# A transformer block with cross-attention on one Trainium2 core: two output tiles moved ahead of the gated layer, and a norm's steps put into every second half unit

## The chip, the cores and the metric

The kernel runs on one core of a Trainium2 chip. The metric is the time of one execution in device microseconds (us). A core has five engines that each work through their own instructions in order: TensorE (PE; its weight loads are PEld), VectorE (DVE), ScalarE (ACT), GpSimd (POOL) and SyncE (SP, which here only starts transfers). They wait for each other by semaphores.

## The reference

The input x has 2 batches of 1024 tokens with 256 features, the context has 2 batches of 154 tokens with 192 features, and all numbers are float32. The block is self-attention, cross-attention and a gated feed-forward layer, each behind a layer norm and each added back to x:

```python
h = _layernorm(x, ln1_g, ln1_b)
x = _attention(h, h, sa_wq, sa_wk, sa_wv, sa_wo, sa_bo) + x
h = _layernorm(x, ln2_g, ln2_b)
x = _attention(h, cond_emb, ca_wq, ca_wk, ca_wv, ca_wo, ca_bo) + x
h = _layernorm(x, ln3_g, ln3_b)
p = h @ ff_w1 + ff_b1
a, gate = (p[..., :D_FF], p[..., D_FF:])
h = a * jax.nn.gelu(gate, approximate=False) @ ff_w2 + ff_b2
return h + x
```

Attention has 16 heads of 64, and D_FF is 1024.

## The kernel before, in words

The order of every instruction is written out by hand: Python closures issue the work, and a few lists hold pieces that are waiting for a place. `tc.manual_schedule()` keeps that order on each engine.

The work has three stages. Self-attention runs in 16 units (2 batches by 8 pairs of heads). Cross-attention follows as 48 steps c, three to a unit. The gated layer follows as 64 half units k (line 1274), with c = 48 + k. The names that matter:

- **The gated layer.** Its tokens are worked in 4 pairs of 256-token blocks, and each pair in 8 units of 128 hidden features; a unit is two half units. The products of a unit are arranged so that seven matrix products of 256 columns serve both token blocks, at the price of sums made ahead: `weight_sums` (L956) and, once for each pair, `token_sums` (L976, four POOL additions L982 to L985). `gate_first` (L1003) issues product 1 into the bank `pa`, then `gate_last` of the unit before (L1045: its last product, into its `pb`), then products 6 and 5 into new `pb` and `pc`. `gate_second` (L1030) adds products 2, 7 and 3 to `pa`, `pb` and `pc`. Beside them stand, for each unit, three ACT instructions (L1018, L1036, L1042), five on DVE (L1022, L1024, L1038, L1041, L1050) and two POOL multiplications (L1043, L1052). They work in a tile `own`, taken from the pool `pp_`, which has 6 buffers and also holds attention weights `p`, the token sums `hs` and the normalised rows `xn`.
- **Results of the gated layer.** From unit 8 on, two product steps `sum_slot` (L1058, output `pf`) are issued in each half unit.
- **What is left of cross-attention.** The weighted values of the last two units of cross-attention (`cross_values`, L861, output `poc`, units 14 and 15) fall into half units k = 1 and k = 5. Their DVE copies go into `o_ca` (L890).
- **Output tiles of cross-attention.** `out_piece` (L457) issues four matmuls of 256 columns into a bank `py_ca`, for two token tiles, and leaves a DVE addition to x (L470) in the list `adds`. Four such pieces make up one quarter (`half`) of the heads for a batch. `out_pieces` puts them in the list `outs`. Quarter 2 of batch 1 needs `o_ca` up to unit 13, quarter 3 up to unit 15.
- **The last norm.** `norm_beside("ff", 1)` (L322), called at k = 7, puts seven steps in the list `side`. A step does, for different pairs of token tiles, the transposition `turn` (four PE transpositions L276 into a bank `ph`, then two ACT instructions L291), `stats` (DVE, L236 and L237, twice), `deviation` (POOL, L242 and L246) and `normalize` (DVE L252, then two POOL instructions L263 that write `xn`). The transposition of a pair comes one step after its `normalize`. An eighth item, `add_biases`, puts eight POOL additions of a bias (L316) in the list `later`. One item is popped from `later` per half unit. The last transposition of batch 0's norm is still in `side` when the gated layer begins.
- **Filling.** At the end of each half unit `run_work(n, n_side, bank, n_sum)` (L559) takes up to `n_side` items from `side`, and up to `n` output tiles from `outs` into banks of the pool `ps_m` (`mm_tile`), with `n_sum` more into banks of the pool `ps_o` (`sum_tile`). A step with transpositions needs a bank: it takes one of the `n`, or `bank` when that is given.
- **The seam.** Before the gated layer the score banks' pool `ps_s` is closed and a pool `ps_f` of four banks opened in its place (L1271 to L1273); `pb` and `pc` come from it. They so follow the last exponentials (ACT, L814) that read the scores of step 47.

The lines that the change touches, before:

```python
if k == 0:
    out_pieces("ca", B - 1, NQ - 2, out_order("ca"))
...
run_work(0 if k == 1 else 1 + k % 2, 1, sum_tile if len(CG) + 2 < k < 2 * NF else None)
```

Of the kernel before, what the change touches and what calls it, by code (L numbers as in the profile page):

```python
# [18 lines left out]
def tile_transformer_block(ctx: ExitStack, tc: tile.TileContext, a: dict, out: bass.AP):  # L19
# [4 lines left out]
    B, S, D = x.shape  # L24
# [5 lines left out]
    NQ = 4  # L30
# [21 lines left out]
    NF = DF // P  # L52
# [45 lines left out]
    for n in names:  # L98
        k = n_of[n]
# [200 lines left out]
    def tile_order(kind):  # L300

        if kind == "ff":
            return list(range(NT))
        return [t for i in range(NT // 2) for t in (i, NT // 2 + i)]
# [17 lines left out]
    def norm_beside(kind, b):  # L322

        after = {"sa": None, "ca": "sa", "ff": "ca"}[kind]
        stats, deviation, normalize, turn = norm_pieces(kind, b)
        n = 1 if narrow(kind, b) else 2
        lag = {}  # L330
        for fns, first in ((turn, 3), (stats, 0), (deviation, 1), (normalize, 2)):
            for i, fn in enumerate(fns):
                t = i if fns is stats else 2 * i + 1
                lag.setdefault(first + t // n, []).append((fn, fns is turn))
        for k in range(NT // n + 3):
            tiles = tile_order(kind)[k * n:(k + 1) * n]
            needs = [(after, b, half, t) for half in range(NQ) for t in tiles if after]

            def step(fns=lag[k]):
                done = [fn() for fn, _ in fns]  # L340
                return next((fn for fn in done if fn), None)

            side.append((any(turns for _, turns in lag[k]), needs, step))
        if not narrow(kind, b):
            side.append((False, (), lambda: add_biases(kind, b)))
# [111 lines left out]
    def out_piece(kind, b, g, t):  # L457

        o = oT[kind, b, g]
        py = spare["out"](f"py_{kind}{b}_{g}_{t}")  # L460
        for e in range(2):
            for i in range(HP):
                nc.tensor.matmul(  # L463
                    py[:, e * D:(e + 1) * D], lhsT=o[:, i, (t + e) * P:(t + e + 1) * P],
                    rhs=wo[kind][:, g * HP + i, :], start=(i == 0), stop=(i == HP - 1),
                )
        xs = xt[b, t // GT][:, t % GT:t % GT + 2, :].rearrange("p t d -> p (t d)")

        def add():
            nc.vector.tensor_tensor(xs, py, xs, ALU.add)  # L470
            added.update((kind, b, g, t + e) for e in range(2))

        add.adds = True
        return add

    def out_order(kind):

        return [t for t in tile_order("ff" if kind == "ca" else "ca") if t % 2 == 0]
# [67 lines left out]
    stores, adds = [], []  # L546
    later = []

    def run(piece):
        done = piece()  # L550
        if done is not None:
            (adds if getattr(done, "adds", False) else stores).append(done)

    def flush(queue):
        for fn in queue:
            fn()
        queue.clear()

    def run_work(n, n_side, bank=None, n_sum=0):  # L559

        while n > 0 and work:
            n -= work[0].banks
            run(work.pop(0))
        for _ in range(min(n_side, len(side))):
            needs_bank, needs, fn = side[0]
            if needs_bank and not bank and n <= 0 or not added.issuperset(needs):
                break  # L570
            if needs_bank and not bank:
                n -= 1
            spare["bank"] = bank or mm_tile
            run(fn)
            side.pop(0)
        for i in range(min(max(n, 0) + n_sum, len(outs))):
            spare["out"] = mm_tile if i < n else sum_tile
            run(outs.pop(0))

    def out_pieces(kind, b, half, tiles):  # L580
        outs.extend(lambda t=t: out_piece(kind, b, half, t) for t in tiles)
# [120 lines left out]
    CG = [(t, min(TG, NT - t)) for t in range(0, NT, TG)]  # L702
# [144 lines left out]
    def cross_regroup(c):  # L847

        ui, n = divmod(c - len(CG) - 2, len(CG))
        if n != 0 or not 0 <= ui < NU:  # L850
            return
        for a2 in range(2):
            for a4 in range(P // KB):
                half, e = divmod(a4, 2)
                own = slice(a4 * KB, (a4 + 1) * KB)
                src = slice((2 * half + a2) * KB, (2 * half + a2 + 1) * KB)
                blocks = pTc["ring"][src, ui % 3, :2 * NM].rearrange("p (m e) j q -> p m e (j q)", e=2)
                nc.sync.dma_start(
                    out=pTc["pairs"][own, a2].rearrange("p m j q -> p m (j q)"), in_=blocks[:, :, e])
# [47 lines left out]
    def cross_drain(c):  # L907

        n = c - 2
        if 0 <= n < CA:  # L910
            cross_turn(n)

    def cross_weigh(c):

        ui, n = divmod(c - 2 * len(CG) - 1, len(CG))
        if n == 0 and 0 <= ui < NU:
            for part in range(2):
                run(lambda: cross_values(ui, part))
            flush(stores)
# [56 lines left out]
    def token_sums(pair):  # L976

        b, t0 = divmod(pair * 2 * BT, S)
        h = hT["ff", b]
        own = [[h[:, c, t0 + j * BT:t0 + (j + 1) * BT] for j in range(2)] for c in range(NC)]  # L980
        t = pp_.tile([P, 3, BT], F32, tag="P", name=f"hs{pair}")
        nc.gpsimd.tensor_tensor(t[:, 0, :], own[0][1], own[0][0], ALU.subtract)  # L982
        nc.gpsimd.tensor_tensor(t[:, 1, :], own[1][1], t[:, 0, :], ALU.subtract)
        nc.gpsimd.tensor_tensor(own[0][1], own[1][1], own[0][1], ALU.subtract)
        nc.gpsimd.tensor_tensor(t[:, 2, :], own[1][0], t[:, 1, :], ALU.subtract)  # L985
        wh[pair] = {
            1: own[0][0], 2: own[1][0], 3: own[1][1], 4: t[:, 2, :],
            5: t[:, 0, :], 6: t[:, 1, :], 7: own[0][1],
        }
# [92 lines left out]
    with tc.manual_schedule():  # L1082
# [98 lines left out]
        for c in range(CA):  # L1181
# [89 lines left out]
        scored.close()  # L1271
        pools["f"] = ctx.enter_context(
            tc.tile_pool(name="ps_f", bufs=4, space=bass.MemoryType.PSUM))  # L1273
        for k in range(2 * FU):
            c = CA + k
            flush(adds)
            (gate_second if k % 2 else gate_first)(k // 2)
            flush(stores)
            flush(lates)
            if k == 2 * len(CG) + 1:  # L1280
                norm_beside("ff", B - 1)
            if k == 0:
                out_pieces("ca", B - 1, NQ - 2, out_order("ca"))
            cross_drain(c)
            if k % 2:
                cross_weigh(c - 1 if k == len(CG) + 2 else c)
            cross_regroup(c)
            if k == len(CG) + 2:
                out_pieces("ca", B - 1, NQ - 1, out_order("ca"))
            if k % (2 * NF) == NF and k < 2 * FU - 2 * NF:  # L1290
                token_sums(k // (2 * NF) + 1)
            for _ in range(min(2, len(sums))):
                run(sum_slot)
            flush(stores)
            run_work(0 if k == 1 else 1 + k % 2, 1, sum_tile if len(CG) + 2 < k < 2 * NF else None)
            if later:
                later.pop(0)()
        gate_last(FU - 1)
# [36 lines left out]
```

## Time and profile before

| what | value |
|---|---|
| median of three runs | 1108.2 us (1106.76 to 1109.0) |
| the profiled execution | 1109.85 us |
| its span, first to last instruction | 1108.1 us |
| mean granted clock of TensorE | 0.995 |
| PE busy in the span | 1081.6 us, 98% |
| POOL busy | 734.0 us, 66% |
| first `pa` of the gated layer | 916.58 us from the span's start |
| first `pf` | 978.25 us |

The gated layer takes the last 191 us of the span. In the views, times are us from the span's start. In the timeline a row is a run of like instructions: start, duration, engine, line, operation, output and inputs, count, and in brackets the idle time of the engine just before it with what seems to have ended it. In the view by windows each engine has its busy time in a stretch, and PEclk is the share of full speed that TensorE's clock was granted in it.

### The profile page before, as it was taken

To read this page: it belongs to the slowest core of one execution; us is meant where nothing else is said; L and a number is where in the kernel's file an instruction comes from. 1 tells how busy PE (TensorE), PEld (TensorE's weight loads), DVE (VectorE), ACT (ScalarE), POOL (GpSimd) and SP (SyncE) were. 2 spreads that over 40 slices of the span, in tenths; PEclk is the share of its full clock that TensorE was granted. 3 is DMA by queue.
4 is the path that set the end of the run, shared out by engine and by line. 5 is a ranking of instruction groups with operands and counts; after the bars stand their busy time and mean duration, and the time that the engine had idled before them with its cause. 6 is when DMAs were issued, how large, how long until landed. Compare 5 with 4: busy or idle time off the path is not lost.

```text
span 1108.1 us, 44904 instructions
## 1 busy us (share of the span) xinstructions
PE 1081.6 (98%) x18388; PEld 718.1 (65%) x18388; DVE 894.2 (81%) x1301; ACT 637.8 (58%) x2057; POOL 734.0 (66%) x1552
## 2 busy tenths in 40 slices
PE   8999999999999999999999999999999999899998
PEld 6555666556756555566565565566766677688887
DVE  5889999898988998999998989878777885544442
ACT  4766666766666666666666766665556553132221
POOL 2767777777778777777777767776656784564331
PEclk9999999999999999999999999999999999999999
DMA  3222212121112021111110111046665543000000
GB/s 82 71 56 56 57 28 52 41 53 42 34 42 49 14 48 37 26 42 33 33 42 23 41 33 27 23 99 162 162 160 138 118 110 77 0 8 12 15 15 29
DMA packets 104094, 60.71 MB, mean 55 GB/s; under 512 B 32330, under 2 KB 94674, under 8 KB 103890
## 3 DMA queue, kind: packets, MB, share of 16 engines
q1 hardware_dynamic: 102514, 57.07, 21.8%
q8 instruction: 145, 2.38, 0.9%
q10 hardware_dynamic: 1376, 0.79, 0.2%
q14 instruction: 59, 0.48, 0.1%
HBM read 27.91 MB, written 2.10 MB: 27 GB/s over the span
## 4 chain that ended last, share of the span: by engine, by line
PE 60%; ACT 10%; DMA 8%; DVE 7%; POOL 6%; SPq 4%; issue 4%; DVEq 0%; POOLq 0%; ACTq 0%
PE s L489 10%; PE po L535 10%; ACT p L500 8%; DMA st<-st 6%; PE pf L1065 5%; DVE st L650 5%; PE py_ca L463 4%; PE pq_ca L358 4%; SPq L510 4%; PE poc L877 4%; PE pb L999 4%; PE py_sa L463 3%; PE sc L798 3%; PE pk_sa L358 3%; PE pa L999 2%
## 5 line engine op out<-in xcount | busy, mean ns | idle before, releaser
L500 ACT ACTIVATE p<-s,st 128x512 f32<-128x512 f32 x512 | 345.4, 687 | 195.6 <-DVE st L650 191.9
L600 POOL TENSOR_SCALAR p<-p,rd,ee 128x512 f32<-128x512 f32 x512 | 387.7, 773 | 47.2 <-DVE rd L596 46.2
L650 DVE TENSOR_REDUCE st<-s 128x2 f32<-128x1024 f32 x256 | 300.8, 1216 | 22.8 <-PE s L489 8.2
L614 DVE STREAM_TRANSPOSE pT<-p 128x1024 f32<-128x1024 f32 x256 | 302.3, 1218 | 0.3 <-POOL p L600 0.3
L489 PE MATMUL s<-k_sa,q_sa 64*32 64x512 f32 x4096 | 261.4, 593 | 7.9 <-ACT p L500 7.0
L535 PE MATMUL po<-pT,v_sa 64*32 64x256 f32 x8192 | 240.6, 376 | 1.9 <-DVE pT L614 1.4
L535 PEld LDWEIGHTS po<-pT,v_sa 64*32 64x32 f32 x8192 | 175.7, 106 | 74.8 <-issue 22.0
L489 PEld LDWEIGHTS s<-k_sa,q_sa 64*32 64x32 f32 x4096 | 82.3, 106 | 111.7 <-ACT p L500 54.6
L814 ACT ACTIVATE p<-sc,neg 128x154 f32<-128x154 f32 x256 | 96.4, 406 | 84.0 <-DVE rden L822 78.9
L825 POOL TENSOR_SCALAR p<-p,rden 128x154 f32<-128x154 f32 x256 | 97.4, 402 | 58.5 <-DVE rden L822 58.2
L500 ACT ACTIVATION_READ_ACCUMULATOR p<-s,st 128x1 f32 x512 | 104.0, 203 | 0.0
L523 POOL TENSOR_TENSOR zz<-ee,st 128x8 f32<-128x8 f32 x128 | 26.0, 203 | 72.0 <-ACT ee L521 72.0
L389 PEld LDWEIGHTS pv_sa<-sa_wv,hT_ln 64*128 64x128 f32 x1024 | 58.8, 188 | 14.6 <-issue 5.9
L389 PE MATMUL pv_sa<-sa_wv,hT_ln 64*128 64x128 f32 x1024 | 62.1, 275 | 0.3 <-ACT v_sa L398 0.3
L518 POOL TENSOR_TENSOR dd<-st 128x8 f32<-128x8 f32 x128 | 25.9, 202 | 53.6 <-DMA st<-st 49.1
L463 PE MATMUL py_ca<-ca_wo,o_ca 128*128 128x256 f32 x256 | 59.9, 382 | 0.5 <-DVE o_ca L890 0.5
L463 PE MATMUL py_sa<-sa_wo,o_sa 128*128 128x256 f32 x256 | 59.7, 385 | 0.0
L463 PEld LDWEIGHTS py_sa<-sa_wo,o_sa 128*128 128x128 f32 x256 | 47.3, 190 | 17.9 <-ACT v_sa L398 6.7
L358 PE MATMUL pq_sa<-hT_ln,sa_wq 64*32 64x512 f32 (+1 forms) x976 | 58.4, 587 | 0.0
L358 PE MATMUL pq_ca<-hT_ln,ca_wq 64*128 64x512 f32 (+1 forms) x304 | 57.9, 590 | 0.0
L358 PE MATMUL pk_sa<-hT_ln,sa_wk 64*32 64x512 f32 x960 | 57.4, 590 | 0.5 <-ACT q_sa L373 0.5
L803 DVE TENSOR_REDUCE neg<-sc 128x6 f32<-128x924 f32 (+1 forms) x48 | 47.9, 999 | 11.8 <-PE sc L798 11.7
(117 smaller groups left out, 1464.3 us busy)
## 6 DMA issues: line engine op xcount, KB each, us to landing
wf<-pT_ca SPq DMA_DIRECT2D x128, 128.0 KB, 2.4
st<-st SPq DMA_DIRECT2D x512, 1.0 KB, 1.8
v_sa<-v_sa SPq DMA_DIRECT2D x32, 256.0 KB, 3.8
sa_wq<-in_L_xattn_sa_wq_dram SPq DMA_DIRECT2D x32, 128.0 KB, 3.4
sa_wk<-in_L_xattn_sa_wk_dram SPq DMA_DIRECT2D x32, 128.0 KB, 2.9
sa_wv<-in_L_xattn_sa_wv_dram SPq DMA_DIRECT2D x32, 128.0 KB, 3.1
ca_wq<-in_L_xattn_ca_wq_dram SPq DMA_DIRECT2D x32, 128.0 KB, 3.7
wf<-in_L_xattn_ff_w_dram SPq DMA_DIRECT2D x12, 256.0 KB
```

The lines of the kernel that those rows point to most:

```text
L358: nc.tensor.matmul(pq[r][f:f + m, at:at + n], lhsT=wt[own, c, f:f + m], rhs=h[own, c, t0:t0 + n], start=(c == 0), stop=(c == NH - 1), tile ...
L389: nc.tensor.matmul(pv[r][:, i * P:(i + 1) * P], lhsT=h[own, c, i * P:(i + 1) * P], rhs=wt[own, c, :], start=(c == 0), stop=(c == NH - 1), ...
L463: nc.tensor.matmul(py[:, e * D:(e + 1) * D], lhsT=o[:, i, (t + e) * P:(t + e + 1) * P], rhs=wo[kind][:, g * HP + i, :], start=(i == 0), st ...
L489: nc.tensor.matmul(sc[a4 * KB:(a4 + 1) * KB, j, :], lhsT=q[r, c:c + KB], rhs=k[r, h * HB:(h + 1) * HB], start=True, stop=True, tile_positi ...
L500: nc.scalar.activation(pr[:, j, :], sc[:, j, :], AF.Exp, bias=st[:, 0, 0, i, j:j + 1], accum_out=st[:, 0, 1, i, j:j + 1],)
L535: nc.tensor.matmul(po[a2][d:d + KB, :QH // 2], lhsT=v[r, t, e, d:d + KB], rhs=pT[r, d // DH * NK + n, :], start=(t == 0 and e == 0), stop= ...
L600: nc.gpsimd.tensor_scalar(pr[:, j, :], pr[:, j, :], rd[:, c:c + 1], ee[:, 0, c:c + 1], op0=ALU.mult, op1=ALU.mult,)
L614: nc.vector.transpose(halves[h][:, :, c:c + KB], groups.pop(0).rearrange("p j (n k) -> p (j n) k", k=KB))
L650: nc.vector.tensor_reduce(st[:, 0, 0, i, :], sc[i], AX.X, ALU.max, negate=True)
L814: nc.scalar.activation(pr_[:, j, i, :T], sc[:, j, i * T:(i + 1) * T], AF.Exp, bias=neg[:, j, i:i + 1], accum_out=den[:, j, i:i + 1],)
L825: nc.gpsimd.tensor_scalar(pr_[:, j, i, :T], pr_[:, j, i, :T], rden[:, j, i:i + 1], 1.0, op0=ALU.mult, op1=ALU.mult,)
L999: nc.tensor.matmul(into[:, :BT], lhsT=lhs, rhs=wh[pair][i], start=first, stop=True, skip_group_check=True)
```

## The change

Two edits, both in the gated layer's loop. The four output pieces of quarter 2 are listed before the loop, and in k = 0 two of them are issued ahead of the first unit, into `sum_tile` banks. `run_work` at the end of a half unit now takes an item of `side` only where k is odd, and never passes a bank, so that a step with transpositions uses one of the `n` banks of `mm_tile`.

```diff
+        out_pieces("ca", B - 1, NQ - 2, out_order("ca"))
+        flush(adds)
         for k in range(2 * FU):
             c = CA + k
+            if k == 0:
+                run_work(0, 0, n_sum=2)
             flush(adds)
             (gate_second if k % 2 else gate_first)(k // 2)
             flush(stores)
             flush(lates)
             if k == 2 * len(CG) + 1:
                 norm_beside("ff", B - 1)
-            if k == 0:
-                out_pieces("ca", B - 1, NQ - 2, out_order("ca"))
             cross_drain(c)
...
-            run_work(0 if k == 1 else 1 + k % 2, 1, sum_tile if len(CG) + 2 < k < 2 * NF else None)
+            run_work(0 if k == 1 else 1 + k % 2, k % 2)
             if later:
                 later.pop(0)()
```

The built order of instructions shows what this moves. No engine gains or loses an instruction, and the order of SP's transfers is the same.

| | before | after |
|---|---|---|
| output tiles of quarter 2 | one in k = 2, two in k = 3, one in k = 4 | two ahead of the first `pa`, one in k = 0, one in k = 2 |
| last transposition of batch 0's norm | k = 0 | k = 3 |
| the eight bias additions for batch 0 | k = 1 to 8 | k = 5 to 12 |
| seven steps of the last norm | k = 7, 8, 9, 10, 11, 12, 13 | k = 7, 9, 11, 13, 15, 17, 19 |
| its four transpositions | after k = 10, 11, 12, 13 | after k = 13, 15, 17, 19 |
| the eight bias additions for batch 1 | from k = 14 | from k = 21 |

## The prediction

> **What bounds the kernel now.** I read the page first, then the view by windows over the gated layer's start, then what TensorE waited for there, then the timeline. The page names the bound:
>
> ```profile
> PE 1081.6 (98%) x18388; PEld 718.1 (65%) x18388; DVE 894.2 (81%) x1301; ACT 637.8 (58%) x2057; POOL 734.0 (66%) x1552
> ```
>
> TensorE is busy for 98% of the span. The change neither adds nor removes an instruction, so it can only win back time that TensorE waits or runs slowly. From 914 to 990 us TensorE's waits are these (waiter, waited for, us in total, times, longest), and after 990 us the same view lists none:
>
> ```profile
> PE ph_ln L276 <- POOL xn_ln L263: 5.6, 4, 3.9
> PE pb L999 <- POOL p L825: 2.0, 1, 2.0
> PE py_ca L463 <- DVE o_ca L890: 0.5, 1, 0.5
> ```
>
> Two places carry nearly all of it, the seam (2.0 us) and the last norm's transpositions (5.6 us). Each has a second price, which the windows show in PEclk:
>
> ```profile
> core 0: us, PE busy (x) PEld busy (x) DVE busy (x) ACT busy (x) POOL busy (x), PEclk, DMA share, GB/s
> 915.60:919.00 3.40, 1.68 (x14) 0.86 (x10) 2.80 (x6) 1.58 (x10) 2.96 (x8) 1.00 0.92 198
> 919.00:922.40 3.40, 3.12 (x9) 2.58 (x10) 1.46 (x5) 1.73 (x4) 2.08 (x6) 0.50 0.49 105
> 960.00:963.40 3.40, 0.27 (x1) 0.14 (x1) 2.89 (x9) 0.00 (x0) 3.24 (x7) 1.00 0.01 2
> 963.40:966.80 3.40, 3.19 (x10) 2.61 (x10) 0.48 (x1) 0.47 (x1) 2.88 (x6) 0.50 0.00 0
> ```
>
> After each stretch in which TensorE was busy for half the time or less, the next 3.4 us ran at half clock. The products there start 0.86 us apart instead of 0.43. Such a stretch costs up to 1.7 us.
>
> The Trainium skill ("TensorE: Matmul & The Clock Gate", section "Why this matters for your kernels") asks for no idle gaps over about 3 us. By that rule the 2.0 us gap at the seam would cost no clock, and the sum below would be 1.6 us smaller; the row at 919.00 speaks against the rule. Its Part 1 calls the window of 3413 ns free-running, so that the same gap need not halve the clock in every run; one trace cannot show that.
>
> **The seam.** The view puts `pb`'s wait down to POOL's L825, which was still running. The program's order says that `pb` needs the bank of step 47's scores, whose last reader on ACT is this:
>
> ```profile
> 918.97 0.21 ACT L814 ACTIVATION_READ_ACCUMULATOR p<-sc,neg 128x1 f32 x1
> 919.28 1.19 PE L999 MATMUL pb<-hs,w1s 128*128 128x256 f32 x2 [2.00 <-POOL p L825]
> ```
>
> It ends at 919.18. Work on TensorE ahead of `pb` hides that wait if it can start early. An output tile takes 1.73 us (start at 929.11, the next product at 930.84), two take 3.46. They need `o_ca` of unit 13, whose last DVE copies L890 (915.59, 0.80 us for two) end at 916.4; the old first `pa` had the same wait, with TensorE's whole queue behind it, and its weight load was held up by 0.16 us. So they start at 916.6, `pa` follows at 920.0 and `pb` at 920.5, 1.3 us after ACT is done. What goes:
>
> - from `pa`'s end at 917.01 (916.58 + 0.43) to 919.28: **2.27 us**;
> - the half clock at 919.0 to 922.4: products 919.28 to 922.62 take 3.34 us. The same `pb`, `pc`, transposition and `pa` take 4 x 0.43 = 1.73 at full clock. **1.6 us**;
> - unit 14's `poc` took from 923.58 to 927.28, 3.70 us; unit 15's, with the wait for `o_ca` behind it, 3.33 (940.43 to 943.76). The excess of **0.4 us** is a weight load that waited for ACT L291, the copy of the transposition in k = 0. That transposition moves to k = 3, and the bank's reader is then a DVE addition that is ready before L1038.
>
> Sum **4.2 us** (2.27 + 1.6 + 0.4, rounded). What the edit adds on other engines is off the path. The two additions L470 (0.69 us each) stand on DVE ahead of L1022, which the first `pb` needs no earlier than 921; the second tile ends near 920.0, so its addition ends near 920.7. At worst the second one delays the first products by its 0.69 us; I take 0. Unit 15's transfers (L858) start when `poc` of unit 14 has read the old data. Their last one starts at 929.6 and takes 2.4 us to land, 4.7 us behind that `poc`'s end at 927.3. The new order has 14 products, one tile and one transposition until unit 15's `poc`, 6.06 + 1.73 + 0.43 = 8.2 us (four tiles and 13.0 us before). So 3.5 us of slack remain; I take 0, and the bound above is the 0.4 us that a wait for such a transfer cost at 914.41.
>
> **The last norm.** Count from unit 3's last product, at 954.23 (the first `pb` after the `pa` at 953.80), to the first `pf` at 978.25: 24.02 us. The work in between is 31 products (3 + 3 of unit 4, 7 each of units 5, 6 and 7, 4 of unit 8) and 4 transpositions at 0.43 each, 15.15 us. So **8.87 us** are lost now, 1.7 of them by the half clock. What the first transposition waits for is GpSimd's queue:
>
> ```profile
> 955.42 0.73 POOL L1052 TENSOR_TENSOR u<-own 128x256 f32<-128x256 f32 x1 [0.70 <-DVE own L1050]
> 956.12 0.73 POOL L982 TENSOR_TENSOR hs<-hT_ln 128x256 f32<-128x256 f32 x1
> ...
> 958.30 0.73 POOL L985 TENSOR_TENSOR hs<-hT_ln,hs 128x256 f32<-128x256 f32 x1
> 959.10 0.19 POOL L242 TENSOR_SCALAR var_ln<-mv_ln 128x2 f32<-128x2 f32 x1
> 959.38 0.71 POOL L246 TENSOR_TENSOR rstd_ln<-var_ln,power 128x2 f32<-128x2 f32 x1
> 960.05 0.72 POOL L316 TENSOR_TENSOR x<-x,ff_b 128x256 f32<-128x256 f32 x1
> 960.74 0.73 POOL L1043 TENSOR_TENSOR kT<-own 128x256 f32<-128x256 f32 x1
> 961.54 0.19 POOL L242 TENSOR_SCALAR var_ln<-mv_ln 128x2 f32<-128x2 f32 x1
> 961.82 0.71 POOL L246 TENSOR_TENSOR rstd_ln<-var_ln,power 128x2 f32<-128x2 f32 x1
> 962.52 1.10 POOL L263 TENSOR_SCALAR xn_ln<-x,rstd_ln,off_ln 128x256 f32<-128x256 f32 x2
> ```
>
> There is no gap in it: from 955.42 to the first transposition at 963.13 are 7.71 us of GpSimd, and 955.42 itself is 1.19 us behind the product at 954.23. Spreading the steps gives TensorE more work ahead of the transposition, but **GpSimd gets more too**. In the new order the queue from unit 3's L1052 to the first `xn` holds all of these and also two more bias additions (batch 0's stand at k = 5 to 12 now), unit 4's L1052 and unit 5's L1043. Each steps 0.69 us (960.05 to 960.74): 4 x 0.69 = 2.76. So the first transposition can start 1.19 + 7.71 + 2.76 = 11.66 us after that product. TensorE has 20 products until then (3 + 3, and 7 each of units 5 and 6), 8.66 us: **3.0 us lost**. Some 0.8 of it shows earlier, as waits of second half units for DVE: a step's `stats` hold DVE for 1.08 us (956.07 to 957.15) and now stand ahead of L1050 and L1022, which had 0.2 us to spare (L1022 ended 955.78, product 7 started 955.96).
>
> From the first transposition to the second's first: GpSimd has the second half of `xn` (0.45), two bias additions, L1052, L1043 (2.76), the step to L242 that is 0.11 longer than 0.69, L242 and L246 (0.28 + 0.70) and half an `xn` (0.61), together 4.91. TensorE has the transposition with its wait for the second half of `xn` (963.13 to 963.67, then 0.32) and 7 products (3.03), 3.89. **1.0 us lost**, and 0.43 (0.54 less the 0.11 that one transposition takes) for the split of each of the two. The third and fourth stand behind `pf` work and without bias additions ahead of them; I take 0 for their waits, the bound above is the 1.3 us of the third one now. Sum lost: 3.0 + 1.0 + 2 x 0.43 = **4.9**.
>
> The new first wait leaves 2.2 + 0.4 us idle close together, about the 2.0 us that halved the clock at the seam, so I give a half-clock stretch 7 in 10. Of its 1.7 us the wait of 1.0 that follows absorbs 1.0, so 0.7 x 0.7 = 0.5. Gain 8.87 - 4.9 - 0.5 = **3.5 us**.
>
> **Sum.** 4.2 + 3.5 = 7.7 us from the profiled execution's 1109.85 gives 1102.2. That execution is 1.65 us above the median of the runs shown, about one half-clock stretch. Taking all 7.7 from 1108.2 gives 1100.5; without the seam's 1.6 it gives 1102.1. I predict **1102 us**.
>
> **Rivals.** Measurement can tell 0.2% (2.2 us) from no change, so faster means below 1106.0 and slower above 1110.4.
>
> - *GpSimd keeps up* (7%): the waits for `xn` vanish and only DVE's 0.8 stays. Gain 4.2 + 8.07 = 12.3, 1097.6. Against it: the queue above has no gap, and its items can be counted.
> - *Only the seam gains* (15%): GpSimd's lag takes back the whole 3.5. 1109.85 - 4.2 = 1105.6. For it: GpSimd has 4.9 us of work in each of units 4 to 6 (two multiplications 1.4, two additions 1.4, a norm step 2.0) against TensorE's 3.03.
> - *The seam's wait only moves* (10%): the tiles start late, or `pb` waits for DVE. 1109.85 - 3.5 = 1106.3. Against it: the same `o_ca` was there for `pa` at 916.58.
> - *Slower* (8%): GpSimd paces TensorE through `own`. Of 6 buffers, two hold `hs` and one `xn`, which now lives two half units. If a new unit's L1018 must wait for a late L1052, TensorE follows the queue to its end: 1.19 us, 10.5 to the first `xn`, 4.9 to the second, 3.6 to the third (L1052 and L1043 1.5, L242 and L246 1.0, `xn` 1.1), then 4.8 for 11 products to `pf`. That is 25.0 against 14.3 of work (31 products, 2 transpositions). Lost 10.7, and with four half-clock stretches, half of them absorbed, 14.1, which is 1.0 more than the 13.1 lost now: 1111. It decides once unit 7's L1018 waits past its product 2. Counted from the first transposition, unit 5's L1052 ends at 0.45 + 0.69 + 0.73 = 1.87 and L1018 0.4 later, 2.3; product 2 is due at 0.54 + 0.32 + 4 x 0.43 = 2.6. Only 0.3 us are to spare.
>
> The forecast has 60%, at 1102 and within about 1099 to 1105. Range **1099 to 1106.5**: it takes in the first case, both one-sided gains, and leaves out about 2 in 10. Faster: 0.60 + 0.07 + 0.11 + 0.03 = 0.81; same 0.11 (rest of the two one-sided cases); slower 0.08.
>
> **What would show it.** Right: no wait of the first `pb`, full clock there; the first transposition after k = 13 waits about 2 us and the second about 1 us for `xn`, with GpSimd busy without a gap from its token sums on; the first `pf` near 970 (954.23 - 4.2 + 14.3 + 4.9 + 0.5). Wrong: a wait of the first output tile; waits of `pa` or of product 2 for L1018; no wait for `xn` at all; any new wait behind the first `pf`.

## The result and the profile after

The changed kernel took **1099.66 us** (median of 4 runs, 1098.1 to 1100.75) against 1107.48 us for the kernel before (4 runs, 1106.61 to 1109.0): ratio 0.9927, 95% interval 0.9908 to 0.9946. The forecast was 1102. Measured again beside later experiments, it took 1100.87 us (6 runs) against 1107.65 (16 runs): 0.9946, interval 0.9929 to 0.9963.

The profiled execution took 1098.87 us, its span 1097.1 us, with a granted clock of 0.998. The page of the changed kernel, its row for the bounding engine:

```profile
PE 1076.0 (98%) x18388; PEld 711.9 (65%) x18388; DVE 893.2 (81%) x1301; ACT 638.1 (58%) x2057; POOL 730.1 (67%) x1552
```

The instructions are as many as before. PE is busy for 5.6 us less (1081.6 before). Of these, 2.9 us lie in the part that the change reorders (185.5 us busy from 904.85 to the end, 188.4 from 907.46 before), 1.6 of them by the half clock at the seam. The other 2.7 lie ahead of it, where the order is the same. What TensorE waits for from 905 to 990 us in the changed kernel (waiter, waited for, us in total, times, longest):

```profile
PE ph_ln L276 <- POOL xn_ln L263: 1.8, 1, 1.8
PE pa L999 <- DVE o_ca L890: 0.5, 1, 0.5
PE py_ca L463 <- DVE o_ca L890: 0.5, 1, 0.5
PE pb L999 <- DVE own L1022: 0.4, 1, 0.4
PE poc L877 <- issue: 0.2, 1, 0.2
```

`pb`'s 2.0 us at the seam is gone, and 5.6 us for `xn` have become 1.8. Behind 990 us the view lists none, as before. The windows of the changed kernel, two at the seam and two at the first transposition:

```profile
core 0: us, PE busy (x) PEld busy (x) DVE busy (x) ACT busy (x) POOL busy (x), PEclk, DMA share, GB/s
913.70:917.10 3.40, 3.40 (x18) 2.97 (x17) 2.61 (x5) 1.59 (x8) 3.16 (x9) 1.00 0.94 202
917.10:920.50 3.40, 3.40 (x17) 3.01 (x16) 2.69 (x6) 1.66 (x2) 1.80 (x6) 1.00 0.29 61
955.00:958.40 3.40, 1.72 (x7) 0.82 (x5) 2.90 (x9) 0.98 (x2) 3.24 (x7) 1.00 0.00 0
958.40:961.80 3.40, 2.86 (x8) 2.23 (x9) 0.39 (x3) 0.54 (x2) 3.40 (x6) 0.53 0.00 0
```

At the seam TensorE is now busy throughout, at full clock. At the transposition it is idle for half of a window, and the next 3.4 us run at half clock. The seam in the timeline of ACT, then of PE:

```profile
916.13 0.21 ACT L814 ACTIVATION_READ_ACCUMULATOR p<-sc,neg 128x1 f32 x1
```

```profile
913.74 3.72 PE L463 MATMUL py_ca<-ca_wo,o_ca 128*128 128x256 f32 x16
917.30 0.59 PE L999 MATMUL pa<-hT_ln,wf 128*128 128x256 f32 x2
917.73 0.59 PE L999 MATMUL pb<-hs,w1s 128*128 128x256 f32 x2
```

The last exponential's sum ends at 916.34, and `pb` needs the bank only at 917.73, 1.4 us later. The two tiles (16 matmuls) fill the time. GpSimd's queue ahead of the first transposition, in its timeline:

```profile
948.45 0.73 POOL L1052 TENSOR_TENSOR u<-own 128x256 f32<-128x256 f32 x1 [0.70 <-DVE own L1050]
949.13 0.73 POOL L982 TENSOR_TENSOR hs<-hT_ln 128x256 f32<-128x256 f32 x1
...
955.80 0.73 POOL L316 TENSOR_TENSOR x<-x,ff_b 128x256 f32<-128x256 f32 x1
956.49 0.72 POOL L1043 TENSOR_TENSOR kT<-own 128x256 f32<-128x256 f32 x1
957.29 0.19 POOL L242 TENSOR_SCALAR var_ln<-mv_ln 128x2 f32<-128x2 f32 x1
957.56 0.70 POOL L246 TENSOR_TENSOR rstd_ln<-var_ln,power 128x2 f32<-128x2 f32 x1
958.27 1.09 POOL L263 TENSOR_SCALAR xn_ln<-x,rstd_ln,off_ln 128x256 f32<-128x256 f32 x2
```

Behind the idle time ahead of 948.45 none is named until `xn`: GpSimd works without a gap. What TensorE does then, in its own timeline:

```profile
958.87 1.44 PE L276 MATMUL ph_ln<-ident,xn_ln 128*128 128x128 f32 x4 [1.78 <-POOL xn_ln L263]
960.11 1.06 PE L999 MATMUL pa<-hT_ln,wf 128*128 128x256 f32 x2
960.96 1.06 PE L999 MATMUL pb<-hs,wf 128*128 128x256 f32 x2
```

The transposition waited 1.78 us for `xn`. Its 1.44 us for four instructions (0.60 for four at full clock), and products 0.85 us apart behind it, are the half clock.

**A yardstick.** Whole times scatter by some us from one execution to the next, much of it ahead of the changed part. So I compare the stretch from the last 16-matmul output product ahead of the last scores (at 907.46 before, 904.85 after) to the end of the span: 200.64 us before, 192.25 after, **8.39 less**. The other 2.6 us by which the two spans differ lie ahead of it, where the order is the same. One part of them is a half-clock stretch near 697 us that the execution of before had. The spans are given to 0.1 us, and the stretch is no finer than that. The 8.39 in pieces:

| piece, by TensorE's starts | before | after | less |
|---|---|---|---|
| 16-matmul product to the first work behind the last scores (`pa` 916.58; tiles 913.74) | 9.12 | 8.89 | 0.23 |
| from there to the last output tile (952.07; 945.09) | 35.49 | 31.35 | 4.14 |
| from there to the first `pf` (978.25; 966.39) | 26.18 | 21.30 | 4.88 |
| from there to the end | 129.85 | 130.71 | -0.86 |

Two transpositions (2 x 0.43) now stand behind the first `pf`, so the norm's piece is 4.88 - 0.86 = 4.02.

Most kernels below gain some 1 us less in their medians than in this stretch (before to after 7.8 and 6.8 against 8.39). The profiled execution of before had half clock at both places; e10 will show that the timed ones need not all have had it. The recorded clocks fit this in part: a half-clock stretch of 3.41 us lowers the mean clock of a span by 0.00154, so the mean of 0.99585 over 39 executions of before means 2.7 such stretches on average by my estimate, and the profiled execution had three. That is some 0.5 us; the rest of the difference stays open.

### The profile page after: what moved, and what is told of

Its sections match the earlier page's. It is cut to its first block, busy times and chain, and to the rows that moved or that the text cites. A ratio compares the mean times of both kernels' runs of the same rounds, so it can differ in the third digit from the quotient of the medians.

```text
span 1097.1 us, 44912 instructions
## 1 busy us (share of the span) xinstructions
PE 1076.0 (98%) x18388; PEld 711.9 (65%) x18388; DVE 893.2 (81%) x1301; ACT 638.1 (58%) x2057; POOL 730.1 (67%) x1552
## 4 chain that ended last, share of the span: by engine, by line
PE 72%; ACT 7%; DMA 5%; DVE 5%; POOL 5%; SPq 3%; issue 3%; DVEq 0%; POOLq 0%; ACTq 0%
PE po L535 14%; PE s L489 14%; ACT p L500 6%; PE pf L1065 5%; PE py_ca L463 5%; DMA st<-st 5%; PE py_sa L463 4%; PE pq_ca L358 4%; PE poc L877 4%; PE pb L999 4%; PE pv_sa L389 3%; PE pk_sa L358 3%; DVE st L650 3%; PE sc L798 3%; SPq L510 3%
## 5 line engine op out<-in xcount | busy, mean ns | idle before, releaser
L500 ACT ACTIVATE p<-s,st 128x512 f32<-128x512 f32 x512 | 344.8, 686 | 195.8 <-DVE st L650 183.2
L535 PEld LDWEIGHTS po<-pT,v_sa 64*32 64x32 f32 x8192 | 173.5, 106 | 75.1 <-issue 20.3
L500 ACT ACTIVATION_READ_ACCUMULATOR p<-s,st 128x1 f32 x512 | 103.8, 203 | 0.0
```

What stands on the lines that cost most here:

```text
L500: nc.scalar.activation(pr[:, j, :], sc[:, j, :], AF.Exp, bias=st[:, 0, 0, i, j:j + 1], accum_out=st[:, 0, 1, i, j:j + 1],)
L535: nc.tensor.matmul(po[a2][d:d + KB, :QH // 2], lhsT=v[r, t, e, d:d + KB], rhs=pT[r, d // DH * NK + n, :], start=(t == 0 and e == 0), stop= ...
```

## The experiments

All twelve profiled executions side by side; each stretch is that of one execution, and only the changed kernel was profiled twice. The stretch is the yardstick above; the clock columns say whether the 3.4 us behind the place ran at half clock.

| kernel | stretch | first `xn` wait | half clock at the seam | at the first transposition | time, runs | ratio to before, interval |
|---|---|---|---|---|---|---|
| before | 200.64 | 3.92 | yes | yes | 1107.38, 23; 1107.65, 16 | |
| after | 192.25 | 1.78 | no | yes | 1099.66, 4 | 0.9927 (0.9908 to 0.9946) |
| e1 seam only | 196.66 | 3.91 | no | yes | 1105.11, 12 | 0.9984 (0.9969 to 1.0) |
| e2 norm only | 197.96 | 1.79 | yes | yes | 1105.9, 12 | 0.9978 (0.9962 to 0.9994) |
| e3 biases early | 189.68 | 0.41 | no | no | 1098.07, 6 | 0.9918 (0.9894 to 0.9942) |
| e4 token sums early | 190.42 | 0.35 | no | no | 1098.09, 6 | 0.9923 (0.9897 to 0.995) |
| e5 one tile | 193.78 | 1.78 | no | yes | 1101.08, 6 | 0.995 (0.9935 to 0.9966) |
| e6 both early | 188.64 | 0.15 | no | no | 1096.41, 5 | 0.9906 (0.9891 to 0.9922) |
| e7 two more additions | 193.86 | 1.52 | no | yes, longer | 1102.68, 9 | 0.9956 (0.9942 to 0.997) |
| e8 after again | 192.25 | 1.78 | no | yes | 1100.87, 6 | 0.9946 (0.9929 to 0.9963) |
| e9 one tile, other bank | 192.59 | 1.78 | no | yes | 1099.84, 1 | |
| e10 norm only, other bank | 195.38 | 1.79 | no | yes | 1104.66, 1 | |

The two medians of the kernel before belong to the runs beside e1 to e4 and beside e5 to e8; the ratios of e1 to e8 are against these, that of after is against its own 1107.48.

### The seam alone (e1)

Against the changed kernel, `run_work` has its old arguments back:

```diff
-            run_work(0 if k == 1 else 1 + k % 2, k % 2)
+            run_work(0 if k == 1 else 1 + k % 2, 1, sum_tile if len(CG) + 2 < k < 2 * NF else None)
```

> The first edit alone: two output tiles ahead of the first unit, the last norm's steps in every half unit as before. My theory (two separate places, whose gains add): the first pb no longer waits and the clock there stays full, but the first transposition of the last norm waits about 3.9 us for xn with a half-clock stretch behind it, as before. Gain 4.2 us on the kernel before (about 1103.3), so 3.6 us slower than the changed kernel. Rival 'only the seam matters': the whole gain of 7.8 us is here already, about 1099.7, because GpSimd's queue gives back what the spread wins. Rival 'the clock alone': a gain of 1.7 us or less.

The stretch is 3.98 us shorter than before. The interval of the whole time reaches to no change, so the stretch carries the reading. The timed runs do not confirm the clock part of it: the mean clock is 0.9958 over e1's twelve executions and 0.9960 over the 23 of before beside them, and the profiled one (0.998) is the highest of the twelve. `pb` starts 0.43 us behind `pa` with no wait, and the seam's window is at full clock; the wait for `xn` stays what it was in the kernel before. TensorE's waits from 880 to 1000 us:

```profile
PE ph_ln L276 <- POOL xn_ln L263: 5.2, 4, 3.9
PE py_ca L463 <- DVE o_ca L890: 0.5, 1, 0.5
PE poc L877 <- DMA wf<-pT_ca: 0.3, 1, 0.3
PE poc L877 <- ACT hT_ln L291: 0.3, 1, 0.3
```

The last line is unit 14's weight load, which still waits for the copy of batch 0's transposition. Its transposition stays in k = 0 here, so this term goes with the norm's edit.

### The norm's steps alone (e2)

Against the kernel before, only the arguments of `run_work` are changed:

```diff
-            run_work(0 if k == 1 else 1 + k % 2, 1, sum_tile if len(CG) + 2 < k < 2 * NF else None)
+            run_work(0 if k == 1 else 1 + k % 2, k % 2)
```

> The second edit alone: the last norm's steps in every second half unit, no tile ahead of the first unit. My theory: the first pb waits 2.0 us as before, usually with half clock behind it; the last norm's first transposition waits 2 us for xn instead of 3.9. Gain about 3.5 us on the kernel before (about 1104). Together with the seam alone the two gains make up the whole within 1 us. Rival 'only the seam matters': no gain, within 1 us of the kernel before.

The stretch is 2.68 us shorter, and the first wait for `xn` is the changed kernel's (1.79 against 1.78). The piece from the last output tile (949.71) to the first `pf` (971.33) is 21.62 us. Against 26.18 before and less the 0.86 of the two transpositions that is 3.7 us won. One us of it is lost again earlier, at the third `pa`; the timeline of PE:

```profile
929.60 0.60 PE L276 MATMUL ph_ln<-ident,xn_ln 128*128 128x128 f32 x4
930.04 1.89 PE L463 MATMUL py_ca<-ca_wo,o_ca 128*128 128x256 f32 x8
932.72 0.70 PE L999 MATMUL pa<-hT_ln,wf 128*128 128x256 f32 x2 [0.79 <-DVE x L470]
```

Neither the kernel before nor the changed one has this wait. Added up, the two edits alone give 3.98 + 2.68 = 6.66, together 8.39. e5, e9 and e10 look for the difference.

### Batch 0's bias additions early (e3)

Against the changed kernel, the eight additions of batch 0 move from k = 5 to 12 to k = 1 to 8, so that two of them leave GpSimd's queue ahead of the first `xn`, and two more that ahead of the second:

```diff
+        side.insert(0, side.pop())
         for k in range(2 * FU):
```

> The changed kernel with the eight bias additions for batch 0 on GpSimd where they stood in the kernel before (k = 1 to 8 instead of 5 to 12). My theory: GpSimd's queue paces the last norm, and the change itself lengthened it. Two additions fewer stand ahead of the first xn (1.38 us) and two fewer ahead of the second, so the first transposition's wait falls from 1.8 us to about 0.5, and no half-clock stretch follows. 2 to 3 us faster than the changed kernel (about 1097). Rival 'the chain of the norm's own steps paces it' (DVE's stats, then deviation, then normalize, each a half unit later): the wait stays at 1.8 us and the time at 1099.7.

The stretch is 2.57 us shorter than the changed kernel's. The first wait for `xn` fell from 1.78 to 0.41, that is by two additions (2 x 0.69 = 1.38), and no half clock follows. TensorE's waits for `xn` from 880 to 1000 us:

```profile
PE ph_ln L276 <- POOL xn_ln L263: 0.6, 2, 0.4
```

### The second pair's token sums early (e4)

Against the changed kernel, the four POOL additions for pair 1 move from k = 8 to k = 5:

```diff
-            if k % (2 * NF) == NF and k < 2 * FU - 2 * NF:
+            if k in (NF - 3, 3 * NF, 5 * NF):
                 token_sums(k // (2 * NF) + 1)
```

> The changed kernel with the token sums of the second pair (four GpSimd additions, 2.8 us) at k = 5 instead of k = 8, where GpSimd waits for other engines anyway. My theory: the queue ahead of the first xn is 2.8 us shorter as far as GpSimd was idle before, so the first transposition waits 0.3 us or not at all; the second waits up to 1.0 us, since its own queue is unchanged. 1.5 to 3 us faster than the changed kernel (about 1097.5). Rival 'the norm's own steps': no change, 1099.7.

The stretch is 1.83 us shorter than the changed kernel's. The four additions took 2.87 us of GpSimd ahead of the first `xn` (949.13 to 952.00 in the changed kernel). GpSimd's timeline shows why not all of it is won; in their place it waits for ACT:

```profile
949.50 0.73 POOL L1043 TENSOR_TENSOR kT<-own 128x256 f32<-128x256 f32 x1 [1.23 <-ACT own L1042]
```

2.87 - 1.23 = 1.64 us come through: the wait for `xn` falls by 1.43 (to 0.35) and that for L1022 by 0.16 (to 0.21). Four waits for `xn` remain on TensorE:

```profile
PE ph_ln L276 <- POOL xn_ln L263: 1.5, 4, 0.8
```

The longest (0.77) is now the second transposition's. The half clock had hidden it in the changed kernel; with full clock behind the first transposition, GpSimd is late for the second one, as the prediction had counted (1.0). So e3 and e4 show the same cause by two different works: what leaves GpSimd's queue ahead of `xn` is won on TensorE.

### One tile ahead of the first unit (e5)

```diff
-                run_work(0, 0, n_sum=2)
+                run_work(0, 0, n_sum=1)
```

> Changed kernel with one context output tile ahead of the first unit in place of two; the other one goes back to the later half units. Yardstick: the stretch from the start of the 16-matmul output product (py_ca, x16) that stands some 9 us ahead of the last scores to the end of the span; 200.6 us in the kernel before, 192.3 in the changed kernel. My theory (the seam's gain is the first pb no longer waiting for the exponentials, and the half clock that went with that wait): the exponentials' release lies 3.43 us after the last scores begin (915.85 to 919.28 in the kernel before), a tile fills 1.72 us, scores and pa take 1.15, so pb waits about 0.55 us, which is short of every wait after which the clock was seen halved (1.64 the shortest), and the stretch is 192.8 us; the median stays within 1 us of the changed kernel's. Rival (the gain comes from the work moved ahead, tile by tile, not from the wait): one tile gives about half of the 4.0 us that the seam was worth alone, so 194.3. Second rival (the half clock comes with any wait here): 192.8 plus 1.7, so 194.5, with the granted clock at about 0.7 in a slice near 917 us.

`pb` does start where the exponentials release it, 3.43 us behind the last scores' start (913.02 to 916.45), at full clock. But the stretch is 193.78 us, 1.0 more than my theory said and nearer to the rivals' 194.3 and 194.5. Neither rival's reason holds: the seam's window is at full clock, and the cost lies elsewhere. The timeline of PE has e2's wait once more:

```profile
916.45 0.67 PE L999 MATMUL pb<-hs,w1s 128*128 128x256 f32 x2 [0.28 <-POOL p L825]
...
931.80 0.70 PE L999 MATMUL pa<-hT_ln,wf 128*128 128x256 f32 x2 [0.79 <-DVE x L470]
```

### Both works out of GpSimd's queue (e6)

The edits of e3 and e4 together.

> Changed kernel with both of GpSimd's postponable works taken out of its queue ahead of the last norm: the first batch's bias additions in the half units 1 to 8, and the second pair's token sums at half unit 5. My theory (GpSimd's queue alone makes the last norm's transpositions late): the waits left with one of them alone (0.41 and 0.21 us with the biases early; 0.35, 0.21, 0.77 and 0.21 with the token sums early) go to 0.3 or less together, no half clock follows, and the stretch from the 16-matmul product to the end is 189.0 us (189.7 and 190.4 with one alone, 192.3 in the changed kernel); median about 1096 to 1097.5. Rival (the DVE or ACT steps ahead of the norm now end last): the waits stay at 0.4 to 0.8 us, now put down to VectorE or ScalarE, and the stretch at 189.5 to 190.5. Second rival (the token sums early make another wait in the half units 4 to 6): a wait of 0.7 or more before 945 us and the stretch at 190 or above.

The stretch is 188.64 us (189.0 expected), the median 1096.41. TensorE's waits from 905 to 990 us:

```profile
PE pa L999 <- DVE o_ca L890: 0.5, 1, 0.5
PE py_ca L463 <- DVE o_ca L890: 0.5, 1, 0.5
PE pb L999 <- DVE own L1022: 0.4, 1, 0.4
PE ph_ln L276 <- POOL xn_ln L263: 0.2, 1, 0.2
```

Of 5.6 us waiting for `xn` 0.2 are left, and no window of its execution is below full clock. By its stretch and its median this is the fastest kernel of the study. Its interval (0.9891 to 0.9922) lies below that of the changed kernel in the same batch (0.9929 to 0.9963), but overlaps those of e3 and e4.

### Two additions more for GpSimd (e7)

```diff
                 token_sums(k // (2 * NF) + 1)
+                if k == NF:
+                    for _ in range(2):
+                        nc.gpsimd.tensor_tensor(
+                            ends[:, :BT], ends[:, :BT], ends[:, BT:2 * BT], ALU.add)
```

> Changed kernel with two additions more (128x256, of a tile that nobody reads any more) in GpSimd's queue behind the second pair's token sums, so ahead of the last norm's first step. My theory (GpSimd runs without a gap from the product at 948.45 to the first normalized piece, so what is put into its queue there is late by as much): two times 0.69 us, the first wait of the transpositions goes from 1.78 to about 3.1 us, and the stretch from the 16-matmul product to the end from 192.3 to about 193.7 us, up to 1 us more where the additions make the second transposition late too. Rival (the norm waits for its statistics on VectorE or for the residual sums, and GpSimd only looks busy): the wait stays at 1.8 and the stretch at 192.3.

The stretch is 193.86 us (193.7 expected). The delay did not appear where I had put it: I had expected a wait of 3.1 us for `xn`. The timeline of PE:

```profile
959.86 0.70 PE L999 MATMUL pb<-hT_ln,wf 128*128 128x256 f32 x2 [1.86 <-DVE own L1022]
...
962.77 1.46 PE L276 MATMUL ph_ln<-ident,xn_ln 128*128 128x128 f32 x4 [1.52 <-POOL xn_ln L263]
```

The wait for `xn` is 1.52, but the product before it, which waited 0.37 for VectorE's L1022 in the changed kernel, now waits 1.86. Together 3.38 against 2.15, 1.23 more for additions of 1.37 (2 x 0.69). GpSimd has no gap from 950.86 to `xn`. So GpSimd's delay reaches TensorE by VectorE too. VectorE's timeline shows the way:

```profile
958.41 0.67 DVE L252 SCALAR_TENSOR_TENSOR off_ln<-mv_ln,rstd_ln 128x2 f32<-128x2 f32 x1 [1.02 <-POOL rstd_ln L246]
959.00 0.47 DVE L1050 SCALAR_TENSOR_TENSOR own<-pb,cols,own 128x256 f32<-128x256 f32 x1
959.40 0.41 DVE L1022 TENSOR_TENSOR own<-pb,own 128x256 f32<-128x256 f32 x1
```

The norm's L252 waits 1.02 us for GpSimd's L246, and L1022, which stands behind it, ends at 959.81, just ahead of the product at 959.86. In the changed kernel this L252 (954.89) has no idle time ahead of it. The clock adds to the loss: two half-clock stretches follow each other here, 6.8 us.

### The changed kernel again (e8)

No edit.

> The changed kernel once more, unchanged, beside the others on one chip, with more runs: median 1099 to 1100.5, about 7.5 to 8 us below the kernel before; the wait of 1.8 us before the last norm's first transposition again, with or without the clock at half speed behind it (the longest wait after which it was seen at full speed is 1.83 us, the shortest after which it was halved 1.64), so the stretch from the 16-matmul product to the end at 192.3 us with it and 190.6 without. Where the stretch is neither, something other than this wait sets it.

The stretch is 192.25 us as in the first execution, within the 0.1 us of the reading, with the same waits and the half clock behind the transposition. The median of 1100.87 is 0.4 above what I had written. The whole span was 5.2 us longer than in the first execution (1102.3 against 1097.1), all of it ahead of the stretch.

### The bank of one output tile (e9, e10)

In e5 and e2 the transposition and the output tile of half unit 3 both take banks of `mm_tile`, of which there are two. Only the tile's bank is changed, the order stays:

```diff
-            run_work(0 if k == 1 else 1 + k % 2, k % 2)
+            run_work(0 if k == 1 else 1 if k == 3 else 1 + k % 2, k % 2, n_sum=k == 3)
```

> The kernel with one tile ahead, with one thing changed: the output tile of half unit 3 goes into a bank of the other pool (sum_tile in place of mm_tile); the order of instructions on every engine stays. There the third pa waited 0.79 us for the addition L470 that reads this tile, and started 2.68 us after the tile did, against 1.72 in the other places. My theory (the transposition of half unit 3 and this tile hold both banks of mm_tile, so pa must wait for the tile's addition, and the second tile ahead of the first unit is worth what it is because no tile then stands there): the wait goes, pa starts 1.72 us after the tile, and the stretch from the 16-matmul product to the end goes from 193.78 to 192.8 us. Rival (VectorE itself is late there, whatever the bank): the wait and 193.8 stay.

> The kernel with only the norm's steps moved, with the same change of bank for the first output tile of half unit 3, which now has a bank of the other pool; the order of instructions stays. My theory: its third pa waits no longer (0.79 us in the kernel without this), and the stretch goes from 197.96 to about 197.0 us, up to 0.3 less where the product behind that pa waited for a bank too; so about 1 us of the 1.7 us by which the two edits together gain more than one by one (8.39 against 3.98 and 2.68) is this bank. Rival (VectorE late): 198.0 stays.

In both the wait is gone, and `pa` starts 1.73 us behind the tile (1.72 expected). e9's stretch went from 193.78 to 192.59, 1.19 less (1.0 expected). So the second tile ahead of the first unit is worth what it is because it is out of the way at half unit 3; for `pb` one tile would nearly have done. e10's went from 197.96 to 195.38, 2.58 less, and the bank explains only 1.0 of it. The rest is the clock. `pb` waited 2.00 us as in the kernel before, but e10's windows at the seam are:

```profile
915.60:919.00 3.40, 1.67 (x14) 0.86 (x10) 2.79 (x6) 1.64 (x10) 3.02 (x8) 1.00 0.92 198
919.00:922.40 3.40, 3.12 (x15) 2.79 (x16) 2.25 (x6) 1.72 (x4) 3.02 (x9) 1.00 0.50 107
```

TensorE is busy for 1.67 of 3.40 us, as before (1.68), and yet the next window is at full clock. The same wait cost the 1.6 us of half clock in two executions (before, e2) and not in this one; the last section shows what differed.

The 1.73 us by which the two edits gain more together than one by one can now be named. In e2 the bank costs 1.0, and a gap of 0.3 ahead of the next tile (934.55 to 934.86) is another loss that the changed kernel lacks. In e1 unit 14's `poc` takes 3.88 us (921.46 to 925.34) against 3.33 in the changed kernel, 0.55 more. That is 1.85.

## Why the prediction was right, point by point

- **What bounds the kernel**: right. No work was removed, and the gain is TensorE's waits and half clock.
- **The seam, 4.2**: 4.14 measured. `pb`'s wait of 2.27 is gone, with 1.4 us to spare (1.3 forecast). Unit 14's `poc` takes 3.33 us, the 0.4 forecast; e1 shows that this term belongs to the norm's edit, since batch 0's transposition leaves k = 0 by it. No wait for L470 or for unit 15's transfers appeared. The second tile's real use, the bank at half unit 3, was not in the prediction.
- **The half clock at the seam, 1.6**: right for the profiled execution, too much as a sure term. Two of three executions with the 2.0 us wait had it. The prediction's reading, that half clock follows a stretch in which TensorE is busy for half the time or less, holds nearly throughout for stretches on a grid that is fixed within an execution (the last section). The same 2.00 us can fall into one such stretch, or into two as in e10.
- **The norm, first transposition**: forecast 11.66 us behind unit 3's last product, 3.0 lost. Measured 958.87 - 947.25 = 11.62, less the 8.66 of products 2.96. GpSimd's queue, counted item by item as 10.47 us from L1052, took 958.87 - 948.45 = 10.42. e3, e4, e6 and e7 show that this queue is the cause, in both directions.
- **The norm, second transposition**: forecast 1.0 + 2 x 0.43 + 0.5 = 2.4 lost. From 958.87 to 964.09 are 5.22 us with 8 x 0.43 = 3.46 of work, so 1.76 lost. This is the term that was mis-sized, by 0.6. The half clock came (7 in 10 forecast) and absorbed not only the wait of 1.0: no split of a transposition is shown in this execution either. The norm is therefore worth 4.02 and not 3.5.
- **First `pf` near 970**: 966.39. The sum behind it gives 969.73; 2.8 of the difference is the earlier start of the whole stretch in this execution, 0.6 the point above.
- **The rivals**: GpSimd did not keep up, and the seam's wait did not move. TensorE was not paced by `own` either: no `pa` and no product 2 waits for L1018 in the changed kernel, though only 0.3 us were to spare by the prediction's count.
- **From the sum to 1102**: the stretch without the 0.23 gained 8.16 us, 7.7 forecast. The choice of 1102 took the seam's half clock out of what the timed runs can win. With all of it, the prediction's own 1100.5 lies between the two measured medians (1099.66 and 1100.87). So 1102 was 1.1 to 2.3 us too high; the 1.6 left out and the 0.5 of the norm are of that size together.

## What to carry to other kernels

Where an in-order engine runs without a gap, the time at which it delivers can be counted item by item to within 0.1 us; spreading its steps helps only if what spreads in between them isn't queued ahead of them too, and moving postponable work out of that queue won another 3.6 us here (192.25 to 188.64). Work put into a hole must be looked at from the place that it left as well: the second tile was worth its 1.0 us there, by a bank. Where whole times scatter, compare a stretch between two fixed instructions; it agreed within 0.1 us in two executions whose spans differed by 5.2.

## What the runs showed of the hardware

For waits of 1.5 to 2 us the length of the wait does not decide whether half clock follows. All twelve executions have the same wait near 695 us, where TensorE's scores wait for the exponentials (L500). Counted over the places:

| place | idle just before | next 3.4 us at half clock |
|---|---|---|
| 720 to 727 us, for `pT` | 1.10 to 1.42 | 0 of 8 |
| 34 us, for ACT L500 | 1.57 to 1.59 | 1 of 12 |
| near 695 us, for ACT L500 | 1.53 to 1.88 | 6 of 12 |
| first transposition, for `xn` (with up to 0.4 shortly ahead) | 1.78 to 1.79 | 6 of 6 |
| seam, for the exponentials | 2.00 | 2 of 3 |
| first transposition, for `xn` | 3.91 to 3.92 | 2 of 2 |

Near 695 us the length does not decide: 1.56 and 1.64 halved the clock, 1.70 and 1.83 did not.

What differs is where the idle time falls on a grid. In all twelve traces, every change of the granted clock within the span lies a whole number of 3.413 us behind the first one. In the kernel before, the half-clock stretches begin at 697.13, 919.00 and 963.37 us, 65 and 13 such steps apart. The windows of e10 on its own grid; half clock would stand in the row behind the one that causes it:

```profile
core 0: us, PE busy (x) PEld busy (x) DVE busy (x) ACT busy (x) POOL busy (x), PEclk, DMA share, GB/s
914.84:918.25 3.41, 2.43 (x28) 1.38 (x18) 2.42 (x7) 1.65 (x10) 3.03 (x8) 1.00 0.72 155
918.25:921.67 3.42, 2.40 (x11) 2.17 (x12) 2.07 (x6) 2.47 (x8) 3.04 (x9) 1.00 0.71 152
921.67:925.08 3.41, 3.41 (x41) 2.45 (x43) 2.93 (x7) 0.98 (x2) 1.55 (x4) 1.00 0.02 5
692.97:696.39 3.42, 1.61 (x26) 0.30 (x28) 3.42 (x4) 2.89 (x10) 2.69 (x6) 1.00 0.03 5
696.39:699.80 3.41, 3.41 (x19) 1.35 (x20) 3.25 (x5) 1.59 (x5) 2.94 (x6) 0.50 0.03 1
```

And near 695 us in the changed kernel's first execution, on its grid:

```profile
692.39:695.81 3.42, 1.88 (x32) 0.37 (x32) 3.32 (x4) 3.29 (x11) 2.34 (x7) 1.00 0.02 5
695.81:699.22 3.41, 2.88 (x24) 1.62 (x24) 3.35 (x5) 1.73 (x5) 3.19 (x6) 1.00 0.03 1
```

At the seam of e10 the 2.00 us fall into two windows of the grid, each busy for 2.4 of 3.4 us. In the kernel before and in e2 they fall into one, busy for 50% and 41%. Near 695 us, 1.56 us of waiting leave 1.61 us busy in e10, and 1.70 leave 1.88 in the changed kernel.

Counted on these grids, the twelve executions have 17 windows at full clock in which TensorE was busy for 48.1% or less, and half clock followed each. Five had 48.7 to 49.6%, and it followed one. It followed none from 52% on. The window in which the program's last matmul ends is left out of these counts: there half clock followed 16 to 38% (four executions) and did not follow 41 and 46% (e2 and before), so the border is not the same everywhere. This rule was found in the same traces that it describes; no run was made to test it. The grid lies differently against the program in each execution (its window at the seam begins 0.3 us ahead of the last scores before, 1.0 ahead in e10, 0.9 behind in e2), so for a forecast such a wait remains a matter of chance.

The Trainium skill ("TensorE: Matmul & The Clock Gate", Part 1) describes a free-running window of 3413 ns, which agrees with the grid and with the 6 of 12. Its rule of no idle gaps over about 3 us (section "Why this matters for your kernels") is too wide here, since gaps of half that length cost up to 1.7 us each.
